# A two-layer model on one core: TensorE adds the last experts' results, tokens are mixed in the weights, and the order is written anew

## The chip, the core and the metric

The kernel runs on one core of one Trainium2 chip. A core has five engines that matter here, each with its own queue of instructions that it works off in order: TensorE (PE, matmuls and transposes), VectorE (DVE), ScalarE (ACT), GpSimd (POOL, which also issues the indirect DMAs) and SyncE (SP, which issues nearly all other DMAs). On-chip memory is SBUF, of 128 partitions; matmuls write to PSUM, of which there are eight banks of 128 x 512 float32. The metric is the time of one execution on the device in microseconds, the median of several runs.

## The reference, cut to what matters

The input x has 4 sequences of 256 tokens, each of width D = 256. Eight blocks follow one another, each adding to x what it computes from the layer-normed x. Everything is float32.

1. A "shift mix" block. With xs the sequence shifted by one token, `k = (x*tmk + xs*(1-tmk)) @ Wk.T + bk`, and in the same way v and r (r with a SiLU on the mix). A recurrence over the tokens then runs with `t = max(u+k, w)`, `e1 = exp(-w-t)`, `e2 = exp(u+k-t)`: `a = e1*a + e2*v`, `b = e1*b + e2`; its output a/b is multiplied by r and goes through Wo.
2. A mixture of 8 experts, one per token.
3. A state-space block of 8 heads.
4. The mixture of 2 again.
5. Causal attention, 16 heads in 4 groups.
6. A mixture of 32 experts, four per token: `y = (silu(x @ gate.T) * (x @ up.T)) @ down.T`, and the token's result is the sum over its four experts of weight times y.
7. Causal attention with a bias that grows with distance.
8. The mixture of 6 again.

## The kernel before, in words

The 1024 tokens form two groups of 512 (g = 0 and 1), each held in SBUF as x[g], four tiles of 128 tokens. Each block exists once per group. The blocks have letters: A shift mix, F and G the small mixture, S state space, a and b the two attentions, e and f the large mixture.

**What sets the order.** Each block is written as a set of generators ("streams"), one per kind of step, and a long string, ORDER, says which stream takes its next step: `f1d` is the `down` stream of block f, group 1, and `*3` three steps. A step is usually one instruction or a handful on one engine. As every engine is in order, the string sets the sequence on every queue, and on SP's and GpSimd's queues that of the DMAs. A second string, BANKS, says which PSUM bank each new matmul result takes. Streams are registered in `shift_mix` (L266 on), `second_ffn` (L971 on) and the main part (L1460 on).

**Normalising.** `norm_steps` (L222) runs at the head of all eight blocks for each group, so sixteen times: statistics on VectorE, a power on GpSimd (L194), then four VectorE operations (L240, one per tile: subtract the mean, multiply by the inverse deviation), eight transposes on TensorE and two copies on ScalarE.

**Shift mix.** `mix` (L288) makes three mixed inputs per group: for each of two halves of the width, ScalarE scales the shifted tokens (L294) and VectorE multiplies and adds (L296). `keys` (L302) multiplies with Wk, then two VectorE operations (L309, L312) form the two exponents, ScalarE takes the exponentials (L316, L318), and VectorE scans over the tokens (L323) and takes a reciprocal (L326). `values` (L328) scans the values (L341), and GpSimd divides (L344). `receive` (L347) multiplies by r.

**The large mixture.** `route` finds the four experts of each token and a row for each of its four copies: expert e has rows 128e to 128e+127 of a buffer in device memory. `send` (L1028) scatters the tokens' normalised rows there, sixteen indirect DMAs of 128 rows on GpSimd. The experts are worked off in sixteen pairs: `fetch` loads a pair's rows (L1060, SP), `turn` transposes them (L1069, L1073), `gate` multiplies with the gate and up weights (L199) and applies SiLU and the product (L1085, L1087), `turn_back` transposes (L1094, L1097), `down` multiplies with the down weights (L1105), copies the result to SBUF (L1109) and stores it (L1111, SP) to another buffer, `done`. When all sixteen pairs are stored, `back` (L1121) fetches for each tile of tokens the rows of its first, second, third and fourth expert, sixteen indirect DMAs per group, into six buffers that are used in turn, and `add` (L1131, VectorE) multiplies each with the token's weight and adds it to x. `leave` stores x (L1369). Buffers that not every token row reaches are filled with zeros early on (`clear`, L1399).

After the list, a check of how full the experts were chooses whether a second, general version of everything is run; with these inputs it is not.

Of the kernel before, what the change touches and what calls it, by code (L numbers as in the profile page):

```python
# [10 lines left out]
F32 = mybir.dt.float32  # L11
I32 = mybir.dt.int32
# [6 lines left out]
P = 128  # L19
D = 256  # L20
# [10 lines left out]
ROWS = E1 * CAP  # L31
NH, HP, NS = 8, 64, 64
# [7 lines left out]
x1 A0n x0 A0n x0 A0n kf*2 A1n x0*2 A0n*3 A1n x1 ls A1n A0n x1 la A0n*4 A0b A0n x1 l1 ks A0n ka  # L40
A1n*2 A0m0*2 A0n A0m1*2 ks*2 A0m0*2 ks A0m2*4 A0m1*2 la*2 A0k1 la*2 A0k1*2 A1n A0k0*3 lf*3 A1n*3
cl A1n*2 A0v0 A0k0 A0v0 cl*2 lf A0k0 A0v0*2 cl lf A0v1 A0k0*3 A1n kf*2 A1n A0m2 A1m0*2 A0k1*2 kf
lf A0v1 A1b A1n A1m0 A0v1 A1m0 A1k0 cl kf A0k1*2 A1m1*3 A0v1 A1k1 A0k1 A0v1 A1m1 lf A0r0 cl A1m2*2
A0r1 A1k1 A0v0 A0r0 A0r1 A0o*3 F0r A0o ls F0r A0o*2 F0r A0o*2 A1v0 F0r ks A1v1 F0r A1k1*3 A1k0*4
F0r*6 A1k0 A1k1 A1k0 F0r*2 A1k1 A1v0*3 A1v1 F0r*3 l1 F0r*3 A1m2*2 ls A1v1*2 k1 F0r F0s*3 A1k0 A1k1
A1m2 A1r0 F0s F0f*2 A1v0 A1r0 A1v1 A1r1*2 A1o*2 F1r A1o*4 F1r A1o*2 ls F1r*5 F0t*4 lf F0e F0f F0t
F1r*5 F0f lf F0e*3 F1r*4 F0r F1r*4 F1w F0e*2 F0t F0e F0t*2 F0e*5 ks F1s*4 F1f*2 F1t*2 F0w F0b
F1e*2 F1t F1f*2 F1e cl F0a F0b F0a S0n*2 F0b F0a F0b F1t*3 F0a F1e*2 S0n*3 F1e*4 F1t*2 F1e S0n*7
F1e k1*2 S0n S0h S0d PS S0h*2 F1e S0h*2 S0d*2 F1b F1a S1n S0d l1*2 S0h*2 S0c l1 S0h*3 S0d F1b F1a
F1b*2 F1a*2 ls S1n*4 S0g*3 S0h*3 S1n*3 S0h S0c S1n S0g*3 S0h*2 S1n S0c*2 S1n*3 S0h*2 cl S0c S0d  # L50
S0c*2 S0d F1r k1*2 S0h*4 S0c*2 S1h S0c*3 S0h*2 S0g*2 S1d*2 S0d S0u*2 S0l S1d*2 S1c l1 S0m S0u*3
S0l S0m S0l*3 S0u S0v S0m S0v S0l*3 S0v*4 S0d S0v*2 S0l S0v S1c*2 S1d*2 S0l*3 S0v S0o S0y l1 S0o
l1 S0u S0o*2 S1h S0l*2 S1h S0y*2 S0u S1d S1u S0y S0m S0l*7 S0z*3 S0l*2 S1c*2 S0z S0l S1g S1h S1g*2
S1c k1*2 S1c S1h S1c S0z*4 S1h S1c*2 S0v S0o S0z*2 S0v S1c cl*3 S1h*2 S1u cl S1h*2 S0z cl S0z*3
S1c S1h*4 S0y l1 S0y S1u S1h*2 S0z S1g S1h S0z*4 S0o S1h*4 S0y S1h S0y S0z*2 G0r*2 S0z S1h S0o S1h
S1d*2 S0o S0z S1l*2 S1m*2 S1l*6 S1m S1l S1u S1l S1v S0z S1v S0z*5 S1l*2 k1 S1u S0z*2 S1v*3 S0z*3
S1u S0z S1o S1m S0z G0r S0z*2 G0r*2 k1 S1v S1y*2 S1v G0r*3 S1v S1o*4 G0r S1l*2 S1y*2 G0r*2 S1z*2
G0r S1g S1v G0r*2 S1z*3 S1o S1z*7 G0r S1z*3 G0r*5 S1g*3 S1v S1l*2 S1z S1u S1l S1u S1l*2 S1v S1l*3
S1z*2 k1 S1z S1y*3 G0s*4 G0f S1l*2 S1y G1r G0f G0t*2 G0f S1o S1v S1o G0f S1z G0t*2 S1z G0e S1z*5
G0t*2 G0e*2 S1z*7 G0w G0e*4 G0t*2 G0e*2 S1z*3 G1r*2 G0e*2 S1z P2 G0e S1z G1r k1 G1r*3 G0b G1r*2  # L60
G0b*3 G1r G0a a0n G0a*2 a0n G1r*2 G0a a0n*2 G1r*5 a0n*5 G1r*3 G1s*4 a0n*4 a0k a0q*6 G1w a0q G1f
G0r G1r G1f a0q a0k a0p k1*2 G1t*3 G1f*2 k1 a0p*4 G1e a0p*2 G1e*2 G1t G1e a0p G1e*2 a0p*2 G1t*2
a0v*2 a0b*2 a0p*4 G1e a0w*4 a0p a0b a0w*2 a0p G1t a0w*2 a0b a0w a0c a0p*2 G1e*2 a0w*2 G1t a0f
a0p*4 G1e*3 a0f*2 a0w*3 a0c a0w*2 a0a a0w*3 a0p*2 a0f G1b a0p*4 a0f G1b a0f G1b a0w*3 a0b*2 a0w*3
G1b a0f G1a a0p a0c a0p a0b a0w*2 a0f a0w a0f a0w*3 a0c a0w G1a*2 cl a1n a0b a0w*5 a0c a0w*2 a1n
G1a a1n*3 cl a0f*3 a1n*4 a1a a1n*4 a0f a1q*3 a0f*3 a0w e0r*2 a0w*2 a1k*2 a0w*4 a1q cl lw a1q*3 a0f
lw*3 a1q a1p*5 lw*3 a0f*4 a0c a0f*3 a1b a1p a0f*4 e0r lw*4 e0r*2 a1b a1v*2 e0r*2 lw a1w*3 e0r*2
a1p*2 a1w*4 a1p*2 a1w*2 e0r*12 e0s a1p*2 e0s*4 a1c a1f*2 a1p*3 lw a1f e0s*2 a1p a1b*2 e0s a1p*2
a1w*5 a1c a1w*6 a1p*3 a1w*3 a1f*2 a1c e0s a1p*4 e0s a1f*4 e1r e0s*2 e0r e0s*3 a1p a1b*2 a1p a1w
a1f*2 a1w a1p*2 a1w a1f e0s e0f a1p e0f*2 a1w*3 a1c a1b a1w a1f a1w*7 a1c a1b a1w a1f*4 a1w*8  # L70
e0t*4 a1f*2 e0g*3 a1c e0f e0t a1f*5 e0g*2 e0t*2 a1f e0h*2 a1f e0g*3 e0h a1f e0g e1r a1f e1r*3
e0f*2 e1r*4 e0t e0g e0t*2 e0d e0f*2 e0t e0h*2 e0g*3 e0h e1r*5 e0d e1r e0d*3 e0h e0g e0h e0f e0t
e1r e0t*2 e0d*2 e0g e0h e0g e0f e1r*3 e0d*4 e0g*3 e0t*3 e0h e1r*3 e1s*6 e0h*2 e0t e0g*4 e0t*2
e0d*3 e0g*2 e0h e0g*3 e0f e0t*2 e0f*3 e0h*2 e0d*4 e0t*2 e0h e0d e1s e0h*2 e0g e1s*3 e0d e0t e0d*2
e0g e0d*2 e0g e0t e0g*2 e1s*2 e0d*2 e0h*2 e0g e0t*2 e0h*2 e0g*6 e0h e0f*2 e0d*2 e0h e0t e0g e0d
e0g e0t*3 e0d*3 e0g e0h*3 e0d*4 e0h e0d*2 e1s*4 e1f*3 e0g*2 e0h*2 e0d*3 e0g*3 e0h*2 e0d*2 e1t e0d
e1t e0d*2 e1t*2 e0d*2 e0w e0b e1g*4 e0b*2 e1h e0b e1g*2 e0b e1t*2 e1g*2 e0b e1h*3 e1f e1t e1f e1d
e1t e1g*3 e0a e1t e1d e1f*2 e1d*2 e1t e0a*2 e1t e1h e1t e1g*5 e1h*2 e1t e1h e1d e1t e1f*2 e0b
e1d*2 e1h e1d e1g e1d e0a b0n e1g*3 e1t*2 e1d e1f e0b e1h*2 e1f e1d*3 e0b*2 e1h e1d e1g e0a*4
e1g*2 e1t e1h*2 e1g e1d*2 e1t e0a e1g e0b e1d e1g*2 b0n e1t e0b e1h e1t*3 e0a e1g e0b*2 e0a*4 e1h  # L80
b0n e0b*2 e1f e1t e1f*3 e0a e1h e1g e1d*4 e1t*2 e1g e1d e0a b0n*2 e1h e1g b0n e1t e1h b0n*2 e1g*5
e1t*2 e1g b0n*2 e1f b0n e1d b0n*2 e1h b0q e1d*3 e1h*2 b0q e1h b0a b0q e1t*2 e1w e1t e1g*2 e1d*5
b0q b0k*2 e1h b0q*4 e1d e1h*2 b0p*4 e1g*3 e1d*3 e1g*2 e1d*3 e1t e1h*2 b0p*4 e1d e1g e1d*2 b0v*2
e1g*3 e1h*2 b0b*2 e1h*2 b0p e1d*7 b0w b0p*2 b0w*2 b0p*2 b0w*2 b0p*3 b0b b0p*4 b0w*4 b0b e1b e1a
b0c e1b*3 b0p*3 b0w*5 e1b b0c b0f e1a*3 b0f e1b*2 e1a e1b b0p*2 e1b*2 b0b*2 e1a b0w*3 b0f b0w
e1a*3 b0w*2 b0p*4 b0w*4 b0c e1a b0w e1b*3 b0w*5 b0f*2 e1b*2 b0f b0p b0f*4 b0b e1b b0b b0w*3 e1a
b0c b0w*2 f0r b0w*5 b0f b0c e1a*2 b0w b1n*3 b0w b0f b0w*4 e1a*3 b0f b1n*2 b0f f0r b0f*3 b1n b0c
b1n*3 b0f b1a b0f*6 b1n*3 b0f b1n b1k*2 b0f*3 f0r*2 b1q*3 f0r b1q f0r b1q*4 b1p f0r*4 b1p f0r*2
b1p*4 f0r*4 b1b*2 b1w*9 b1v f0r*3 b1p f0r*2 f0s*6 b1p*2 f0s*2 b1v b1p*2 b1c b1p f0r b1p*4 f0s
b1b*2 b1f*3 b1w*5 b1p*3 b1w*2 b1p*4 b1c f0s b1f b1w*7 f0s*2 b1p*5 f0s*2 b1c f0s b1b*2 b1f*2 f0s  # L90
f0f b1f*4 f0f b1w*9 b1c b1w*2 b1f b1w*2 b1p b1f b1p b1w b1b*2 b1w*3 f0f b1w*2 b1c b1w b1f*4 b1w*2
f0t b1f b1w b1c b1f f0w f1r*2 f0t*2 f0g f0t b1f*6 f0g*4 b1f f0h*2 f0g b1f f0t b1f f0f*2 f0t*4 b1f
f1r*3 f0h f0g*4 f0f f0d f0f*2 f1r*4 f0h*3 f0d*2 f0t f1r*3 f0d f1r*2 f0g*2 f0h f1r f0h f0d*4 f1r*3
f0g f0t*3 f1r f0d f0t*2 f0g*3 f0d*2 f0f f0g*2 f0f f0g f1r*2 f0h f0t f1s*2 f0t f0g f0h*2 f1s f0h
f0g*3 f0t*2 f0f*2 f0t*2 f1s f0d f0f f1s*4 f0d*2 f1s f0d*2 f0h f0g*4 f0f f1s*2 f1w f0g f0t*3 f0d
f0h*4 f0g*3 f0d*4 f0f f0d*2 f0t f1s f1r f0h*2 f0f f0g f0h f0t f0g*2 f0d*5 f0g*3 f0h*2 f0t*4 f0d*5
f0h f0g*2 f0t f1s*2 f0g*2 f0h f0d*2 f0g*2 f0h*4 f1s f0d f1s f1f*2 f0t f0d f0g*2 f1f f0g*2 f0d
f0h*2 f0d f0g f0d*4 f1t*2 f0h*2 f1t*2 f1g*2 f1t*2 f1g f1f*3 f0d*4 f1g*2 f0d f0b f1h f1g*2 f1h f1t
f1d f1t f1d f1t*2 f1f f1g*2 f1h f1g*4 f1h*2 f1g*2 f1d f1t*2 f1d f1t f1d f1h f1f f1h f1d f1h f0b
# [12 lines left out]
103675436254102365432651470352147634763405217364053214760765076503762145317624652436517436516742
350361501736540217653402716534071234605137201346720513764051632470562340716523471062345716324057
163240571623405763201574620153467201365247023516702357462513746251740253176253176425031425760314
# [16 lines left out]
def two_blocks(ctx: ExitStack, tc: tile.TileContext, a: dict, out: bass.AP):  # L131
# [86 lines left out]
    def chain(functions):  # L218
        for f in functions:
            yield from f()  # L220

    def norm_steps(g, name, out, dst=None):  # L222


        xg = x[g]
# [1388 lines left out]
```

## Time and profile before

| | us |
|---|---|
| median of 3 runs | 747.05 (745.83 to 756.44) |
| profiled execution, its own time | 747.44 |
| its span, first to last instruction | 745.7 |
| TensorE busy | 618.6 |
| VectorE busy | 477.7 |
| ScalarE busy | 242.4 |
| GpSimd busy | 283.4 |

The profile is of one execution. Its page gives busy times, 40 slices of the span with the busy share of each engine in tenths (9 is 90% or more) and the TensorE clock that was granted, and the costliest groups of instructions; further views give the instructions in order of time, the chain of waits that ended last, sums by window and the DMA queues. In a row such as `x8 | 65.5, 1023` the count is followed by busy microseconds and the mean nanoseconds of one. A float32 matmul appears as two instructions. L numbers are lines of the kernel before.

### The profile page before, as it was taken

To read this page: it belongs to the slowest core of one execution; us is meant where nothing else is said; L and a number is where in the kernel's file an instruction comes from. 1 tells how busy PE (TensorE), PEld (TensorE's weight loads), DVE (VectorE), ACT (ScalarE), POOL (GpSimd) and SP (SyncE) were. 2 spreads that over 40 slices of the span, in tenths; PEclk is the share of its full clock that TensorE was granted. 3 is DMA by queue.
4 is the path that set the end of the run, shared out by engine and by line. 5 is a ranking of instruction groups with operands and counts; after the bars stand their busy time and mean duration, and the time that the engine had idled before them with its cause. 6 is when DMAs were issued, how large, how long until landed. Compare 5 with 4: busy or idle time off the path is not lost. (4 is left out here: it accounts for less than half of the span.)

```text
span 745.7 us, 10482 instructions
## 1 busy us (share of the span) xinstructions
PE 618.6 (83%) x3424; PEld 430.7 (58%) x3424; DVE 477.7 (64%) x1498; ACT 242.4 (33%) x461; POOL 283.4 (38%) x333
## 2 busy tenths in 40 slices
PE   4686869998998798986899989899988889999910
PEld 1253654455666565444458978675446449989910
DVE  7898535797954567566737546458766856645642
ACT  3511214554442123521454323222432255223200
POOL 3223232342653414512730725304841660534344
PEclk9896889999999699995999999899997799999975
DMA  5842358000012123690233767322200124666643
GB/s 163 271 167 93 121 183 295 32 0 1 1 67 81 52 86 127 217 304 22 79 113 107 250 207 237 119 72 75 81 1 2 70 101 126 212 237 223 205 141 103
DMA packets 70829, 94.04 MB, mean 126 GB/s; under 512 B 6896, under 2 KB 60656, under 8 KB 70128
## 3 DMA queue, kind: packets, MB, share of 16 engines
q1 hardware_dynamic: 62944, 72.31, 30.0%
q0 software_dynamic: 7680, 20.98, 8.5%
q8 instruction: 29, 0.48, 0.3%
q14 instruction: 32, 0.26, 0.1%
q10 hardware_dynamic: 144, 0.01, 0.0%
HBM read 50.29 MB, written 42.99 MB: 125 GB/s over the span
## 5 line engine op out<-in xcount | busy, mean ns | idle before, releaser
L199 PE MATMUL pgu_f<-gu,xT_f 128*128 128x192 f32 x512 | 95.7, 333 | 1.7 <-ACT xT_f L1073 1.5
L1121 POOL DMA_INDIRECT yb_f<-done,bk_f x64 | 65.5, 1023 | 72.7 <-DVE x L1131 29.2
L1033 POOL DMA_INDIRECT sent<-xn_f,to_f x64 | 63.0, 984 | 69.0 <-DVE to_f L1021 33.5
L199 PEld LDWEIGHTS pgu_f<-gu,xT_f 128*128 128x128 f32 x512 | 85.0, 194 | 4.6 <-ACT xT_f L1073 3.4
L1105 PE MATMUL py_f<-dw,hT_f 96*128 96x256 f32 x256 | 65.9, 386 | 3.4 <-DVE hT_f L1097 3.4
L1109 DVE COPY ye_f<-py_f 128x512 f32<-128x512 f32 x64 | 43.6, 687 | 28.7 <-PE py_f L1105 18.1
L853 DVE CUSTOM_DVE_ANT_0 junk_a<-pS_a,tri 128x128 f32<-128x128 f32 (+1 forms) x128 | 45.7, 357 | 22.6 <-PE pS_a L843 16.6
L1073 ACT COPY xT_f<-px_f 128x512 f32<-128x512 f32 x64 | 36.8, 587 | 53.3 <-PE px_f L1069 41.8
L853 DVE CUSTOM_DVE_ANT_0 junk_b<-pS_b,tri 128x128 f32<-128x128 f32 (+1 forms) x128 | 45.7, 357 | 12.8 <-PE pS_b L843 6.1
L1105 PEld LDWEIGHTS py_f<-dw,hT_f 96*128 96x128 f32 x256 | 45.4, 192 | 9.3 <-DVE hT_f L1097 4.6
L1085 ACT ACTIVATE he_f<-pgu_f 128x192 f32<-128x192 f32 x64 | 21.2, 332 | 83.9 <-PE pgu_f L199 70.0
L1131 DVE SCALAR_TENSOR_TENSOR x<-yb_f,wt_f,x 128x256 f32<-128x256 f32 x64 | 31.8, 503 | 23.5 <-DMA yb_f<-done,bk_f 22.9
L1087 DVE TENSOR_TENSOR he_f<-he_f,pgu_f 128x192 f32<-128x192 f32 x64 | 22.3, 348 | 28.6 <-ACT he_f L1085 28.5
L891 POOL TENSOR_SCALAR_AFFINE_SELECT pT_b<-pT_b 128x512 f32<-128x512 f32 x32 | 20.6, 672 | 49.5 <-ACT pT_b L888 49.4
L888 ACT ACTIVATE pT_a<-pST_a 128x512 f32<-128x512 f32 x48 | 25.6, 605 | 42.4 <-PE pST_a L880 41.0
L1069 PE MATMUL px_f<-ident,xe_f 128*128 128x128 f32 x256 | 36.9, 273 | 1.6 <-DMA xe_f<-sent 1.6
L1097 DVE COPY hT_f<-ph_f 96x256 f32<-96x256 f32 x64 | 26.1, 415 | 17.5 <-PE ph_f L1094 15.8
L199 PE MATMUL py_f<-W,xT_f 128*128 128x256 f32 x128 | 34.6, 421 | 3.1 <-ACT xT_f L489 3.1
L888 ACT ACTIVATE pT_b<-pST_b 128x512 f32<-128x512 f32 x48 | 25.4, 604 | 30.8 <-PE pST_b L880 25.2
L891 POOL TENSOR_SCALAR_AFFINE_SELECT pT_a<-pT_a 128x512 f32<-128x512 f32 x32 | 19.6, 644 | 37.9 <-ACT pT_a L888 37.9
L1069 PEld LDWEIGHTS px_f<-ident,xe_f 128*128 128x128 f32 x256 | 30.6, 141 | 5.6 <-issue 2.9
L194 POOL TENSOR_TENSOR rstd_f<-var_f,neghalf 128x4 f32<-128x4 f32 x8 | 8.2, 1024 | 66.4 <-DVE var_f L233 66.3
(294 smaller groups left out, 1297.1 us busy)
## 6 DMA issues: line engine op xcount, KB each, us to landing
xe_f<-sent SPq DMA_DIRECT2D x64, 256.0 KB, 3.2
done<-ye_f SPq DMA_DIRECT2D x64, 256.0 KB, 2.5
sent<-nil SPq DMA_DIRECT2D x16, 512.0 KB, 7.8
xe_f<-fsent SPq DMA_DIRECT2D x16, 256.0 KB, 2.9
fdone<-ye_f SPq DMA_DIRECT2D x16, 256.0 KB, 2.1
gu<-in_L1f_gate SPq DMA_DIRECT2D x4, 768.0 KB, 12.8
gu<-in_L1f_up SPq DMA_DIRECT2D x4, 768.0 KB, 17.9
dw<-in_L1f_down SPq DMA_DIRECT2D x4, 768.0 KB, 17.4
```

Of the source, the lines that this page charges most:

```text
L199: nc.tensor.matmul(dst, w(c), rhs(c), start=(c == 0), stop=(c == n - 1))
L853: nc.vector.tensor_tensor_reduce(out=junk[:, :w], in0=four[s][:, at:at + w], in1=tri[:, S - w:], scale=1.0, scalar=NEG, op0=ALU.add, op1=A ...
L888: nc.scalar.activation(pT.rearrange("p c q -> p (c q)"), pS, AF.Exp)
L891: nc.gpsimd.affine_select(pT, pT, pattern=[[0, AG], [1, P]], compare_op=ALU.is_ge, fill=zero, base=0, channel_multiplier=-1)
L1033: nc.gpsimd.indirect_dma_start(out=sent_to[g][t * TOPK + j], out_offset=bass.IndirectOffsetOnAxis(ap=to[:, t, j:j + 1], axis=0), in_=xn[:, ...
L1069: nc.tensor.transpose(px[:, j * P:(j + 1) * P], xe[q][:, k, c * P:(c + 1) * P], ident)
L1073: nc.scalar.copy(xT[q].rearrange("p k c t -> p (k c t)"), px)
L1097: nc.vector.tensor_copy(hT[q].rearrange("p k t -> p (k t)"), ph[:, :2 * P])
L1105: nc.tensor.matmul(py[:, k * D:(k + 1) * D], hT[q][:, k, :], dw[:, 2 * q + k, :], start=True, stop=True)
L1109: nc.vector.tensor_copy(ye.rearrange("p k d -> p (k d)"), py)
L1121: nc.gpsimd.indirect_dma_start(out=yb, out_offset=None, in_=done[g], in_offset=bass.IndirectOffsetOnAxis(ap=kept_["back"][:, t, j:j + 1], ...
L1131: nc.vector.scalar_tensor_tensor(x[g][:, t, :], due[t, j], kept_["wt"][:, t, j:j + 1], x[g][:, t, :], ALU.mult, ALU.add)
```

## The change

It has four parts.

1. **Last group's last eight experts.** `second_ffn` gets an argument `end`; for block f, group 1 it is 8. There, tokens are sent with nine more numbers in their row: the token's number, its four experts and their four weights (buffer `end_sent`, 265 wide). `fetch` also loads those numbers for the rows of experts 24 to 31. `claim` makes from them, for each of the eight experts, a matrix of 128 rows by 512 tokens that holds the weight where the row belongs to the token. The results of pairs 12 to 15 are not stored; `collect` multiplies these matrices with them on TensorE, summed over the eight experts in two PSUM banks, and two VectorE operations add the sums to x. `back` and `add` stay; a copy that went to experts 24 to 31 fetches a row of zeros behind the others (`end_done`).
2. **First block.** The mixing of k and v is moved into the weights: `share` makes tmk*Wk and (1-tmk)*Wk (the same for v) once, on ScalarE, and `mixed` multiplies the tokens with the first and the shifted tokens with the second, four matmuls in place of two. `mix` remains for r. The two exponents are formed by ScalarE as Relu, with changed constants, in place of VectorE.
3. **Normalising.** The four VectorE operations become four of ScalarE with scale and bias; a small VectorE operation makes the bias.
4. **The list.** ORDER and BANKS are new throughout, and the new buffers are zeroed by a new stream, `ce`.

```diff
 def norm_steps(g, name, out, dst=None, xn=None):
+        shift = small.tile([P, NT], F32, tag="shift", name=f"shift_{name}")
+        nc.vector.scalar_tensor_tensor(shift, mv[:, :, 0], -1.0, rstd, ALU.mult, ALU.mult)
...
-            nc.vector.tensor_scalar(
-                xn[:, t, :], xg[:, t, :], mv[:, t, 0:1], rstd[:, t:t + 1],
-                ALU.subtract, ALU.mult)
+            nc.scalar.activation(xn[:, t, :], xg[:, t, :], AF.Identity,
+                                 bias=shift[:, t:t + 1], scale=rstd[:, t:t + 1])
...
+        def mixed(dst, w2, es):
+            xp = kept_["xp"]
+            dst = dst.rearrange("p (b s) -> p b s", b=2)
+            for i, t in enumerate(w2):
+                for c in range(NC):
+                    nc.tensor.matmul(dst, t[:, c, es], xp[:, c, :, 1 - i:S + 1 - i],
+                                     start=(i + c == 0), stop=(i + c == NC))
...
-            nc.vector.tensor_scalar(
-                flat(low), pk, bkuw[:, e:e + 1], 0.0, ALU.add, ALU.min)
-            nc.vector.tensor_scalar(
-                flat(top), pk, bku[:, e:e + 1], w[:, e:e + 1], ALU.add, ALU.max)
+            nc.scalar.activation(flat(low), pk, AF.Relu, bias=minus[:, e:e + 1], scale=-1.0)
+            nc.scalar.activation(flat(top), pk, AF.Relu, bias=bkuw[:, e:e + 1])
...
+                if end and q == 2:
+                    nc.sync.dma_start(
+                        info, sent_[through * 2 * CAP:, D:].rearrange("(k p) d -> p k d", k=end))
...
-                nc.sync.dma_start(rows(done[g], q), ye)
+                if q < through:
+                    nc.sync.dma_start(rows(done_, q), ye)
...
+        def claim():
+            nc.vector.tensor_tensor(
+                mine, info[:, :, 1:1 + TOPK],
+                iota[:, E1 - end:].unsqueeze(2).to_broadcast([P, end, TOPK]), ALU.is_equal)
+            nc.vector.tensor_tensor(mine, mine, info[:, :, 1 + TOPK:], ALU.mult)
+            nc.vector.tensor_reduce(sw, mine, AX.X, ALU.add)
+            for i in range(end):
+                nc.vector.tensor_scalar(
+                    to, numbers, info[:, i, 0:1], sw[:, i, :], ALU.is_equal, ALU.mult)
...
+        def collect():
+            two = [bank(k, f"pend_{name}_{k}") for k in ("acc", "st")]
+            for i in range(end):
+                q, k = through + i // 2, i % 2
+                for t in range(NT):
+                    nc.tensor.matmul(
+                        two[t // 2][:, t % 2 * D:(t % 2 + 1) * D],
+                        due["to", i][:, t * P:(t + 1) * P], due["ye", q][:, k, :],
+                        start=(i == 0 and t % 2 == 0), stop=(i == end - 1 and t % 2 == 1))
+            for t in range(0, NT, 2):
+                xt = x[g][:, t:t + 2, :]
+                nc.vector.tensor_tensor(
+                    xt, two[t // 2].rearrange("p (k d) -> p k d", k=2), xt, ALU.add)
...
+        def share(i, whole, part):
+            for t, by in ((part, tm), (whole, omt)):
+                for c in range(NC):
+                    nc.scalar.activation(t[:, c, :], whole[:, c, :], AF.Copy, scale=by[:, c, i:i + 1])
```

The end of the old list, from the last steps of group 1's products on, and of the new one:

```diff
-... f1h*2 f0b f1d*5 f0a*5 f0b f0a f0b f0a f0b
-f0a f1b*2 z0 f1a*2 f1b f1a f1b*3 f1a*2 z0*3 f1b*2 f1a*3 z1*2 f1b f1a f1b*4 f1a*3 z1 f1a f1b*3
-f1a*3 z1
+... f1d f1g*3 f1h*2 f1t
+f1g*3 f1h*2 f1d*4 f1c*2 f1d f1c f1g*2 f1h f1c f1m*3 f1h*2 f0a f1d*2 f1h f1m f1c f0a f1c f1b*2 f1d
+f1m*2 f1d f1m*3 f1b f1a*3 f1b f1a f1m f1b f1a f1b f1a f1b*5 z1 f1b f1r f1a*6 f1b f1a f1b f1a f1b
+f1a f1b z1*2 z0*2 f1a z1
```

`f1m` is `collect` (eight steps of four matmuls, then the two additions), `f1c` is `claim`, `f1b` a fetch of `back`, `f1a` an addition of `add`.

## The prediction

> **What bounds the kernel now.** First the busy shares in 40 slices of 18.6 us:
>
> ```profile
> PE   4686869998998798986899989899988889999910
> DVE  7898535797954567566737546458766856645642
> PEclk9896889999999699995999999899997799999975
> ```
>
> Three regions: a first block (slices 1 to 6) in which TensorE is half idle and VectorE is the busiest engine; a long middle in which TensorE is at 8 or 9 tenths; and a tail of almost two slices without any matmul. The tail is read from the timeline (start, length, engine, line, operation):
>
> ```profile
> 696.81 1.89 PE L1105 MATMUL py_f<-dw,hT_f 96*128 96x256 f32 x8
> ...
> 711.53 1.13 PE L1105 MATMUL py_f<-dw,hT_f 96*128 96x256 f32 x4 [0.51 <-DVE hT_f L1097]
> 712.70 0.69 DVE L1109 COPY ye_f<-py_f 128x512 f32<-128x512 f32 x1 [0.63 <-PE py_f L1105]
> ...
> 718.21 1.00 POOL L1121 DMA_INDIRECT yb_f<-done,bk_f  x1 [1.59 <-DMA out<-x]
> 719.52 1.00 POOL L1121 DMA_INDIRECT yb_f<-done,bk_f  x1 [0.30 <-issue]
> ...
> 738.08 1.01 POOL L1121 DMA_INDIRECT yb_f<-done,bk_f  x1 [0.30 <-issue]
> ...
> 740.93 0.48 DVE L1131 SCALAR_TENSOR_TENSOR x<-yb_f,wt_f,x 128x256 f32<-128x256 f32 x1 [0.61 <-DMA yb_f<-done,bk_f]
> ```
>
> The last matmul ends at 712.66; then the last results are stored, and sixteen gathers follow at one per 1.31 us. The chain of waits closes it:
>
> ```profile
> 738.08 2.76 DMA yb_f<-done,bk_f
> ...
> 740.93 0.48 DVE x L1131
> ```
>
> A gather takes 2.76 us to land, its addition 0.48, and from 741.41 the output store and the close take 4.3 us to 745.7. Tail: 745.7 - 712.66 = 33.0 us. For the first block I read the sums by window (engines in the order PE, PEld, DVE, ACT, POOL; then clock, DMA share, GB/s) and its timeline:
>
> ```profile
> 25.00:50.00 25.00, 18.07 (x45) 8.64 (x43) 23.26 (x35) 7.64 (x12) 4.43 (x4) 0.86 0.82 275
> 50.00:75.00 25.00, 17.00 (x54) 10.94 (x53) 21.27 (x43) 5.75 (x9) 6.64 (x6) 0.73 0.21 72
> ```
>
> ```profile
> 20.15 1.37 DVE L240 TENSOR_SCALAR xn_a<-x,mv_a,rstd_a 128x256 f32<-128x256 f32 x4
> 21.74 3.60 PE L199 MATMUL pv<-mix,wv 128*128 128x512 f32 x8
> 31.15 6.95 PE L199 MATMUL pk<-mix,wk 128*128 128x512 f32 x8 [5.37 <-DVE mix L296]
> 61.92 6.56 DVE L326 RECIPROCAL sb<-sb 128x512 f32<-128x512 f32 x2
> ```
>
> VectorE has 23 and 21 of 25 us; matmuls wait for its mix.
>
> **Tail, removed and added.** Removed: the stores and fetches of the last four pairs, not the sixteen gathers. All sixteen stay; rows of experts 24 to 31 are merely replaced by one zero row. But they may start when pair 11 is stored. Added on TensorE: 8 experts x 4 tiles x 2 instructions (an f32 matmul shows as two) = 64 of 256 columns. The row at 696.81 gives 1.89/8 = 0.236 us each in a stream: 15.1 us. From below it cannot be less while TensorE is full (25.0 of 25 us busy from 675 to 700); from above each could cost its mean latency, 0.386 us by the group's row: 24.7. I take 0.236, since the rows in question also load a new weight per matmul. Two idle gaps before the last matmuls (0.76 and 0.51 us) get filled. The last matmul, E, moves to 712.66 + 15.1 - 1.3 = 726.5.
>
> What comes after E is decided by order. In the changed program VectorE has: last result copied, first addition of the TensorE sums (waits for the last matmuls), then the sixteen additions of fetched rows. VectorE is in order, and there are six fetch buffers. Six gathers can go early: pair 11's product ends about 25 us before E (three gate groups 4.4, four products 4.1, small transposes, 15.1 of sums), its store lands some 3.5 us on, so they are all done before E. The seventh needs the buffer of the first, whose addition is queued behind the TensorE sums. So the added wait, on VectorE, holds ten gathers on GpSimd. After E: the addition (0.69, begun 0.5 before E, when its bank is complete), 0.48 for the first fetched row: E + 0.7; the tenth gather issued 9 x 1.31 later, E + 12.5; landing 2.76, add 0.48, close 4.3: E + 20.1 = 746.6, against 745.7. **Tail: +0.9 us.** TensorE's 15.1 eats what leaves the tail. Bounds: 0 to +10.5.
>
> **First block.** Off VectorE: 8 mixes x 0.74 = 5.9, 8 key operations of 0.75 and 0.80 = 6.2, four norms x 1.38 = 5.5: 17.6 us. Onto ScalarE: 8 Relu of about 0.72 (the row of mixtmp, L294) for 8 mixtmp taken off; 8 weight scalings and the norms at 0.38 to 0.48 each (ScalarE's 128x256 rows, L933 and L749). ScalarE has 6 to 11 of 25 us there. Onto TensorE: 16 more products of two instructions. By the row at 21.74 an instruction is 3.60/8 = 0.45 us: 14.4; by the row at 31.15, 0.87: 27.8. [...] I take 0.45 to 0.6: 14 to 19 us in a stretch where TensorE has 7 to 8 us idle per 25.
>
> On the chain, mixtmp 0.72 and mix 0.74 go and twice the product (1.8) comes: nothing. What can gain is only VectorE's queue. I followed it through the new order: group 0 leaves attention some 2.5 us sooner, but the second reciprocal of group 1 now stands behind group 0's routing, as the pair at 61.92 did, so group 1 gains 2; and before the state space starts, two expert products stand between its two sets of transposes. Between 0 and -10; I take **-2**, nearest to that walk.
>
> **Norms.** All sixteen: four VectorE operations (1.38) become a small one (0.17) and four of ScalarE (1.5 to 1.9), with one more handoff (about 0.2): +0.5 to +0.95 until the transposes, and behind an exponential (0.605, L888) up to +1.55. In the trace TensorE waited before transposes at 7 of 17 places; elsewhere other work hides it. 7 x 0.75 = 5, less what the freed VectorE returns: **+2** (from -5 to +10). ScalarE also gets four more table loads in the new order (26 for 22), most of them in the state-space stage, 1.28 each in the trace; 5.1 on an engine about half busy there: **+1** (0 to 5).
>
> **A new wait: the token numbers.** The load of 1024 pieces of 36 bytes stands on SP's queue behind the first three fetches of the last group. VectorE's claim waits for it, and behind the claim stand that group's first gate products, for which TensorE's transposes wait. The queue's line
>
> ```profile
> q1 hardware_dynamic: 62944, 72.31, 30.0%
> ```
>
> gives 0.30 x 16 x 745.7 / 62944 = 57 ns of one engine per packet, so 1024/16 x 57 = 3.6 us. [...] Bounds 0 and 5; I take the row's price and **+1**.
>
> **Covered edits.** Clearing the wider send buffer (4.3 MB, nine DMAs) stands on SP's queue before the expert weights. At the best slice's 304 GB/s that is 14 us more. The weights were issued from 304 us on, 9.4 MB or some 31 us, and first used at 382.4: about 47 us of cover; without it, 14. Claims: 8 x about 0.6 on VectorE, which has 9 us free of 25 there; at worst 6. Sends with rows of 1060 bytes instead of 1024, two iotas and casts: nothing. The result: +0.9 - 2 + 2 + 1 + 1 = +2.9 on the profiled 747.44, whose span is 745.7 (the median of three runs, 747.05, is next to it): **750**. The new list rearranges everything else. Between 125 and 700 us TensorE's idle time sums to 56 us; a fair list could win or lose some 8 of it, and I put the mean at nothing.
>
> **Rivals.**
> - *VectorE set the pace.* If the first block passes on 12 of its 17.6, and twelve later norms a third of their 1.2 each (5): 747.4 + 0.9 - 17 = 731. For it: 23.3 of 25 us busy at 25 to 50, 23.4 at 150 to 175. Against: the order of reciprocals, and TensorE's own 14 to 19 there.
> - *Slower: norms wait in ScalarE's queue.* Place: the head of every stage. Price: 1.55 each with an exponential in front. It passes 2% from ten exposed norms on (15.5); with twelve, 18.6: 747.4 + 0.9 - 2 + 1 + 1 + 18.6 = 767. Against: only 7 places waited.
> - *Gathers hidden after all.* If fetched rows were added before the TensorE sums, only the two additions of the sums and the close would follow E, some 5.2 us: 731.7, and with the other +2 and the 1.7 us that lie outside the span 735. The order on VectorE speaks against it; it lies within 2% anyway.
>
> **Numbers.** Forecast, little change, 0.65 (738 to 762); hidden gathers 0.05; VectorE's pace 0.12; ScalarE's queue 0.18. So faster than 2% 0.12, within 0.70, slower 0.18; 2% is about what a measurement of this kernel can tell from no change. Range 735 to 763: it reaches into both outer cases, with the list's 8 and the bounds of norms and first block.
>
> **What would show it.** Last matmul about 14 us later than 712.66; 64 new matmul rows 0.236 us apart; exactly six gathers of the last group before E, ten after it 1.31 apart; end about 20 us after E; VectorE's windows at 25 to 75 down by some 10 us while the first state-space transposes still come near 111. Wrong if the early stages end over 10 us sooner, if TensorE waits before most transposes, or if the gathers run on past E without a pause.

## The result, and the profile after

The changed kernel takes 773.83 us (median of 4 runs, 771.93 to 778.76), the kernel before 750.5 (4 runs, 745.83 to 756.44). The ratio is 1.0345, with a 95% interval of 1.0293 to 1.0396: slower by some 25 us, where 750 was forecast. The profiled execution took 771.93 us, its span is 770.2, 24.5 more than before.

The busy tenths of the changed kernel's page, in slices of 19.3 us, first:

```profile
PE   5968679899998699695989989899997999989990
DVE  3786336487564456647635755658948645645753
PEclk9989789699999699997899999998997599989995
```

VectorE is indeed less busy in the first slices (3 7 8 6 for 7 8 9 8), and the tail without matmuls is now one slice instead of two. Both things happened that the change does on purpose, and still the end is later. The windows view, cut at the same events in both kernels (the last product of the first small mixture; the first transpose of the last group's experts; the last matmul), shows where. The columns are the time on PE, PEld, DVE, ACT and POOL with instruction counts, then granted clock, share of DMA, GB/s. Before:

```profile
0.00:113.40 113.40, 76.29 (x254) 48.69 (x255) 80.34 (x187) 31.15 (x46) 32.31 (x46) 0.85 0.50 166
113.40:611.50 498.10, 443.08 (x2542) 291.07 (x2541) 326.09 (x1127) 177.45 (x342) 200.80 (x237) 0.93 0.32 104
611.50:712.70 101.20, 99.23 (x632) 90.98 (x630) 59.23 (x161) 33.76 (x73) 31.68 (x32) 1.00 0.60 193
```

After:

```profile
0.00:114.50 114.50, 85.04 (x290) 53.09 (x291) 62.60 (x155) 44.24 (x75) 31.84 (x45) 0.90 0.39 136
114.50:630.00 515.50, 455.48 (x2539) 295.23 (x2538) 317.39 (x1102) 203.11 (x385) 202.67 (x241) 0.91 0.36 115
630.00:749.40 119.40, 115.96 (x696) 105.32 (x694) 66.60 (x180) 35.13 (x77) 39.94 (x40) 0.97 0.55 171
```

| stretch | before | after | change | forecast |
|---|---|---|---|---|
| to the last product of the first small mixture | 113.4 | 114.5 | +1.1 | -2 |
| from there to the last group's experts of block f | 498.1 | 515.5 | +17.4 | +3 (norms 2, table loads 1) |
| those experts and the TensorE sums | 101.2 | 119.4 | +18.2 | +14.8 |
| tail behind the last matmul | 33.0 | 20.8 | -12.2 | -12.9 |
| span | 745.7 | 770.2 | +24.5 | +2.9 |

So the forecast missed by 21.6 us, and 14.4 of them are in the middle, a stretch in which the change touches the norms and the list and, beside them, only the clears and the wider rows that are sent. TensorE has nearly the same instructions there (2542 and 2539) but is busy 12.4 us longer at a lower clock (0.91 for 0.93), and idle 5.0 us longer (55.0, now 60.0).

The tail, in the changed kernel's timeline (start, length, engine, line, operation, idle before and its releaser):

```profile
733.83 1.28 POOL L1198 DMA_INDIRECT yb_f<-end_done,bk_f  x1 [6.22 <-DVE ye_f L1148]
...
742.12 1.07 POOL L1198 DMA_INDIRECT yb_f<-end_done,bk_f  x1 [1.75 <-DVE x L1208]
...
748.42 1.03 PE L1181 MATMUL pend_f_st<-ye_f,cw_f 128*128 128x256 f32 x4
748.62 0.69 DVE L1188 TENSOR_TENSOR x<-pend_f_acc,x 128x512 f32<-128x512 f32 x1 [5.35 <-PE pend_f_acc L1181]
749.35 2.05 DVE L1208 SCALAR_TENSOR_TENSOR x<-yb_f,wt_f,x 128x256 f32<-128x256 f32 x4
750.11 1.13 POOL L1198 DMA_INDIRECT yb_f<-end_done,bk_f  x1 [6.92 <-DVE x L1208]
...
762.04 1.17 POOL L1198 DMA_INDIRECT yb_f<-end_done,bk_f  x1 [0.30 <-issue]
```

Six gathers go between 733.83 and 742.12, GpSimd then stands 6.92 us, and ten follow from 750.11, 1.3 apart. VectorE stands 5.35 us before the first addition of the sums with those fetched rows ready behind it. Three rows of the chain of waits:

```profile
119.48 8.66 DMA yb_f<-fdone,bk_f
...
310.77 6.36 DMA yb_f<-fdone,bk_f
...
762.04 3.30 DMA yb_f<-end_done,bk_f
```

It closes as it did before. Its first two rows are gathers of the second group in the first and in the second small mixture; before, the four in each place took 5.7 to 6.6 and 2.8 to 3.8 us to land. The chain of the kernel before leads back only to 734.87, so whether gathers lay on it earlier can't be read.

### The profile page after: what moved, and what is told of

It is laid out like the page before. It is cut to its first block, busy times and chain, and to the rows that moved or that the text cites. A ratio compares the mean times of both kernels' runs of the same rounds, so it can differ in the third digit from the quotient of the medians.

```text
span 770.2 us, 10750 instructions
## 1 busy us (share of the span) xinstructions
PE 656.5 (85%) x3520; PEld 453.6 (59%) x3520; DVE 455.1 (59%) x1455; ACT 282.5 (37%) x537; POOL 284.8 (37%) x335
## 3 DMA queue, kind: packets, MB, share of 16 engines
q1 hardware_dynamic: 67634, 75.65, 30.2%
## 4 chain that ended last, share of the span: by engine, by line
PE 50%; DVE 18%; issue 10%; DMA 9%; ACT 8%; POOL 4%; POOLq 0%; SPq 0%; DVEq 0%; ACTq 0%
PE pgu_f L204 8%; PE py_f L1144 6%; DMA yb_f<-fdone,bk_f 3%; PE px_f L1108 3%; PE pST_b L894 2%; DVE junk_a L867 2%; PE py_f L204 2%; PE pST_a L894 2%; PE pq_a L204 2%; PE pS_b L857 2%; DVE junk_b L867 2%; PE pctx_b L916 2%; PE pctx_a L916 2%; PE po_a L204 2%; PE pob L204 1%
## 5 line engine op out<-in xcount | busy, mean ns | idle before, releaser
L204 PE MATMUL pgu_f<-gu,xT_f 128*128 128x192 f32 x512 | 93.9, 330 | 0.3 <-ACT pT_a L902 0.3
L1198 POOL DMA_INDIRECT yb_f<-done,bk_f x48 | 49.6, 1034 | 58.2 <-DVE x L1208 20.3
L1068 POOL DMA_INDIRECT sent<-xn_f,to_f x48 | 47.3, 985 | 49.2 <-issue 27.9
L1148 DVE COPY ye_f<-py_f 128x512 f32<-128x512 f32 x64 | 43.7, 686 | 29.2 <-PE py_f L1144 16.8
L1208 DVE SCALAR_TENSOR_TENSOR x<-yb_f,wt_f,x 128x256 f32<-128x256 f32 x64 | 31.5, 499 | 13.8 <-DMA yb_f<-end_done,bk_f 7.6
L1136 DVE COPY hT_f<-ph_f 96x256 f32<-96x256 f32 x64 | 26.2, 415 | 21.3 <-PE ph_f L1133 19.4
L905 POOL TENSOR_SCALAR_AFFINE_SELECT pT_a<-pT_a 128x512 f32<-128x512 f32 x32 | 19.7, 638 | 44.9 <-ACT pT_a L902 44.9
## 6 DMA issues: line engine op xcount, KB each, us to landing
gu<-in_L1f_gate SPq DMA_DIRECT2D x4, 768.0 KB, 13.5
```

The costliest lines, as they stand in the source:

```text
L204: nc.tensor.matmul(dst, w(c), rhs(c), start=(c == 0), stop=(c == n - 1))
L905: nc.gpsimd.affine_select(pT, pT, pattern=[[0, AG], [1, P]], compare_op=ALU.is_ge, fill=zero, base=0, channel_multiplier=-1)
L1068: nc.gpsimd.indirect_dma_start(out=sent_to_[t * TOPK + j], out_offset=bass.IndirectOffsetOnAxis(ap=to[:, t, j:j + 1], axis=0), in_=xn[:, t ...
L1148: nc.vector.tensor_copy(ye.rearrange("p k d -> p (k d)"), py)
L1198: nc.gpsimd.indirect_dma_start(out=yb, out_offset=None, in_=done_, in_offset=bass.IndirectOffsetOnAxis(ap=kept_["back"][:, t, j:j + 1], ax ...
L1208: nc.vector.scalar_tensor_tensor(x[g][:, t, :], due[t, j], kept_["wt"][:, t, j:j + 1], x[g][:, t, :], ALU.mult, ALU.add)
```

## The experiments

All were timed beside the kernel before on the same chip, and a ratio is to that kernel. Two of the chips used took 802 and 803 us for the kernel before, not 750, so their ratios are compared only with each other. Where a part is put into the old list, its new steps stand where the new list or the data allow, and the PSUM banks are those of the old list.

### One part at a time in the old list

Norms on ScalarE, with everything else as before:

```diff
-            nc.vector.tensor_scalar(xn[:, t, :], xg[:, t, :], mv[:, t, 0:1], rstd[:, t:t + 1], ALU.subtract, ALU.mult)
+            nc.scalar.activation(xn[:, t, :], xg[:, t, :], AF.Identity, bias=shift[:, t:t + 1], scale=rstd[:, t:t + 1])
```

> The kernel before with one thing done: norms on ScalarE, the small operation put into the old list just ahead of them; old first block, old tail. Theory N: 757 to 767 us. Theory L: 745 to 752. My recorded sum had +2 for it, 749.

Measured: 778.48 us, ratio 1.0394 (1.0267 to 1.0521), above theory N's 757 to 767 too. This one edit alone costs as much as the whole change. As the list is the same, each matmul can be set against its twin, and one jump of the lag is 6.0 us at a single place. Before, around the norms of block e, group 1:

```profile
390.90 0.58 ACT L1073 COPY xT_f<-px_f 128x512 f32<-128x512 f32 x1
...
391.56 1.54 PE L199 MATMUL pgu_f<-gu,xT_f 128*128 128x192 f32 x8
```

and with the norms on ScalarE:

```profile
415.09 1.04 POOL L197 TENSOR_TENSOR rstd_f<-var_f,neghalf 128x4 f32<-128x4 f32 x1 [10.86 <-DVE var_f L236]
416.16 0.16 DVE L241 SCALAR_TENSOR_TENSOR shift_f<-mv_f,rstd_f 128x4 f32<-128x4 f32 x1 [1.15 <-POOL rstd_f L197]
...
416.36 2.07 ACT L247 ACTIVATE xn_f<-x,shift_f,rstd_f 128x256 f32<-128x256 f32 x4 [4.01 <-DVE shift_f L241]
418.34 0.56 ACT L1104 COPY xT_f<-px_f 128x512 f32<-128x512 f32 x1
...
418.95 2.93 PE L202 MATMUL pgu_f<-gu,xT_f 128*128 128x192 f32 x8 [5.88 <-ACT xT_f L1104]
```

The copy needed nothing from the norm: its transposed tokens had lain ready since 410. It stood behind the norm in ScalarE's queue while ScalarE waited 4.01 us for VectorE and GpSimd, and TensorE stood 5.88 us; the matmuls behind ran at half pace (2.93 for 1.54). Before, the first operation behind this norm on VectorE was a copy (L1097), and TensorE did not wait for it.

The same edit, but with each norm's four operations as late in ScalarE's queue as they can stand (in the second group of both attentions they so come behind the addition of the block's bias to x and normalise another x, so that the result is another one; the instructions are as many as before):

```diff
-e1r*4 e0t e0g e0t*2 e0d e0f*2 e0t e0h*2 e0g*3 e0h e1r
+e0t e0g e0t*2 e0d e0f*2 e0t e0h*2 e0g*3 e0h e1r*5
```

> The kernel before with the norms on ScalarE, as in the earlier run, but the four operations of each norm as late in ScalarE's queue as they can stand, directly before the norm's transposes, so that copies which TensorE waits for go first. Theory Q (waiting work behind the norms): the two places that gave 4.1 and 6.0 us of the 31 vanish, ratio to the kernel before 1.022 to 1.030 instead of 1.039. Theory D (only the norm's own length counts): 1.035 to 1.045.

Measured: 764.08 us, ratio 1.0198 (1.0123 to 1.0272), on theory Q's side and a little below its band. Half of the price went away with the place in the queue, more than the two places named. Lag of the last transpose of some norms behind the kernel before, in us (third row: the doubled norm of the next section):

| time before | 52.9 | 134.2 | 254.3 | 336.3 | 397.2 | 481.0 | 565.0 | 625.5 |
|---|---|---|---|---|---|---|---|---|
| norms on ScalarE | 7.8 | 13.0 | 13.5 | 21.3 | 29.9 | 27.0 | 32.7 | 31.6 |
| the same, late | 4.3 | 6.7 | 7.2 | 15.8 | 16.8 | 16.0 | 19.7 | 18.2 |
| VectorE's norms twice | 9.8 | 12.4 | 17.6 | 24.4 | 26.7 | 25.4 | 30.2 | 31.6 |

The lag grows in steps spread over the program, and little of it is won back. These are profiled executions; that of the late placement (766.56 us) was the longest of its four, and by the medians it loses 14 us, not 18.

The first block alone (the scalings in the places of the mixes of k and v, their weights loaded sooner):

```diff
-A1n*2 A0m0*2 A0n A0m1*2 ks*2 A0m0*2 ks A0m2*4 A0m1*2 la*2
+A1n*2 kk*2 A0n kv*2 ks*2 kk*2 ks A0m*4 kv*2
```

> The kernel before with only the new first block (mixing in the weights, Relu on ScalarE), put into the old list: the weight scalings stand where the mixes of k and v stood. Theory F (the first block's doubled products move later stages back by more than VectorE gains): 752 to 758 us. My recorded sum: -2, so 745; the recorded bound of a gain is 737. Theory L: between 740 and 748.

Measured: 751.56 us, ratio 1.0046 (1.0014 to 1.0078): +3.4 us, neither a gain nor the loss of theory F.

The new end alone:

```diff
+    if end and q == 2: nc.sync.dma_start(info, ...)
-    nc.sync.dma_start(rows(done[g], q), ye)
+    if q < through: nc.sync.dma_start(rows(done_, q), ye)
+streams[n + "c"] = claim(); streams[n + "m"] = collect()
```

> The kernel before with only the new end of the last group (rows with token numbers, claim, collect, sixteen gathers of which experts 24 to 31 fetch a zero row), put into the old list near the same steps as in the new one. Recorded sum: +0.9 for the tail and +1 for the token numbers, so 749; last matmul near 727, end 20 us after it. If instead the last experts' stretch lengthens by 18 us as it did in the changed kernel (119.4 for 101.2), 753.

Measured: 767.32 us, ratio 1.02 (1.0081 to 1.032), worse than the sum. Its wide clears ran at 295 to 310 us, and there the gathers of the second small mixture took 5.9 to 7.7 us (before: 2.8 to 3.8). With the clears early, and the last gathers and their additions laid among the last products:

```diff
-cl ce*9
+ce*9 G0f
...
-f1d f1m f1c*2 f1d f1m*2 f1d f0a*5 f0b f0a f0b f0a f0b f0a f1b*2 f1m*3 f1b f1a*3 f1b
+f1a f1b f1a f1b f1d f1m f1c*2 f1a f1b f1d f1m*2 f1a f1b f1d f1m*2 f1a f1b
```

> The kernel before with the new end of the last group in its old list, the gathers interleaved with the last products as above, and the wide buffer cleared early, near 120 us, instead of at 295. From 747: TensorE's added 15.9 and some 2 of drift, less the tail that shrinks from 33 to about 12: 742 to 748. If the clears at 295 to 315 us were not what delayed that kernel's middle (its lag grew from 2.8 to 9.8 us there): 748 to 756.

> The kernel before with the new end of the last group alone, gathers interleaved, early clears. On the slow chip it reached the third block's norms at the time of the kernel before (330.7 for 331.8 us). Theory: the tail alone, placed so, is worth a little: 740 to 747, up to 1% below the kernel before. If TensorE's 16 us eat it all: 747 to 752.

Measured on the slow chips: ratios 0.9965 (0.9919 to 1.0011) and 0.9982 (0.993 to 1.0034). Placed well, the new end costs nothing and brings nothing that can be told from no change. It is the best version found, and it does not beat the kernel before. Early clears and interleaved gathers were not tried apart.

All three parts in the old list, clears early:

> All three parts of the change in the old list (norms on ScalarE, new first block, new end as in the changed kernel, clears early). If the parts add up (3.9% for the norms, 0.5% for the first block, 0 to 2% for the end): ratio 1.045 to 1.065, and the new list of the changed kernel (1.0345, and 1.019 on the slow chip) has won back 1 to 4% of it. If instead the new list is what costs: ratio 1.00 to 1.03.

Measured: 791.08 us, ratio 1.0548 (1.0463 to 1.0632). The parts add up (3.9 + 0.5 + 0 to 2), and the new list with the same parts is at 1.0345. So for these parts the new list is not the cause of the loss: it wins two points back. With norms on VectorE it does not win, as shown below.

### How open a norm's time is

The norm's four operations twice, with the same result:

```diff
+            nc.scalar.activation(xn[:, t, :], xg[:, t, :], AF.Identity, bias=shift[:, t:t + 1], scale=rstd[:, t:t + 1])
             yield
```

> The changed kernel with each normalising operation of ScalarE issued twice (same result): 64 more of 0.55 to 0.59 us, 2.3 us per norm, 37 in all. Theory N (the norm's time on ScalarE lies open at most of the sixteen places): 25 to 40 us slower, 799 to 813. If it is covered at most places, as my recorded sum had it (7 of 16): 10 to 17 us, 784 to 791. Theory L, norms next to nothing: under 8, below 781.

> The kernel before with each normalising operation of VectorE issued twice: 64 more of 0.345 us at full pace, 1.4 us per norm, 22 in all. If a norm's time is as open before as after the change: 15 to 24 us slower, 763 to 772. With 7 of 16 open: 10, 757.

Measured: the changed kernel goes to 829.27 us (ratio 1.1088, 1.0907 to 1.1269), 55 more; the kernel before goes to 779.1 (1.0412, 1.0288 to 1.0536), 29 to 31 more. Both are above what was expected of fully open norms (799 to 813 and 763 to 772). How much longer one norm became has to be read from its rows. VectorE, before and doubled (first and last of eight rows):

```profile
7.57 1.38 DVE L240 TENSOR_SCALAR xn_a<-x,mv_a,rstd_a 128x256 f32<-128x256 f32 x4 [0.17 <-POOL rstd_a L194]
...
7.43 0.41 DVE L240 TENSOR_SCALAR xn_a<-x,mv_a,rstd_a 128x256 f32<-128x256 f32 x1 [0.17 <-POOL rstd_a L194]
...
10.20 0.41 DVE L243 TENSOR_SCALAR xn_a<-x,mv_a,rstd_a 128x256 f32<-128x256 f32 x1
```

ScalarE, changed and changed with doubled norms:

```profile
76.82 2.08 ACT L249 ACTIVATE xn_f<-x,shift_f,rstd_f 128x256 f32<-128x256 f32 x4 [2.39 <-DVE shift_f L243]
...
85.99 0.60 ACT L249 ACTIVATE xn_f<-x,shift_f,rstd_f 128x256 f32<-128x256 f32 x1 [2.39 <-DVE shift_f L243]
...
90.00 0.60 ACT L251 ACTIVATE xn_f<-x,shift_f,rstd_f 128x256 f32<-128x256 f32 x1
```

On VectorE the four operations went from 1.38 us to 3.18: 1.80 more, not the 1.38 that was expected: the eight operations start 0.40 us apart on the mean (10.20 - 7.43 over seven), not 0.345. Sixteen times that is 28.8 us, and the kernel takes 29 to 31 longer, so on the whole a lengthening is paid once, in full. On ScalarE they went from 2.08 to 4.61, sixteen times 40.5, and the time grew by 55, 1.4 us for each. So the norms as a whole are covered in neither kernel; that not a single one is covered isn't shown. What the changed kernel pays on top goes with a lower clock: over the stretch to the last matmul it is granted 0.92 and with doubled norms 0.88, and TensorE's busy time goes from 656.5 to 681.6 us for the same instructions.

### Norms back on VectorE in the new list

> The changed kernel with one thing undone: the four normalising operations of each norm are VectorE's again (the step of the small operation is empty); new list, new first block, new tail. Theory N (the norms on ScalarE cost the 18 us that the body lost): 756 to 762 us, and the first matmuls of the last experts near 615 instead of 630. Theory L (the new list costs them, the norms next to nothing): 768 to 776, the last experts' first matmuls at 626 or later.

Measured: 781.7 us, ratio 1.0401 (1.0289 to 1.0513), slower than theory N and L alike expected. The list had put the norm's steps where ScalarE was free, and on VectorE other work came between them: one norm ended 13.5 us after GpSimd began its power and another 8.3, where the kernel before has 2.5 at most places. So the steps were moved together (theory N below still takes 1.4 us of time for each us of a norm; the rows above give about 1.0 for VectorE's):

```diff
-S1n S0h*2 S1n*2 k1*2 S1n*2 S0c*3 ls S0g
+S1n*5 S0h*2 k1*2 S0c*3 ls S0g
```

> The changed kernel with the norms back on VectorE as in the run before, and besides the four operations of each norm directly behind one another at the place of the small operation (in the earlier run they stood where the list had put them for ScalarE, and VectorE's own work came in between). Theory N (a norm's length lies open at every place, at 1.4 us of total time per us): norms shorter by 1.0 to 1.5 us at sixteen places, 752 to 762 us. Theory L (the new list is slow by itself): 768 to 782.

> Norms on VectorE and close together, in the new list. On the slow chip it brought the last matmul 5.5 us forward against the kernel with norms on ScalarE there. Theory N in full (all of the body's 18 us are the norms'): 752 to 758. Norms a third of it and the new list the rest, as the slow chip's trace has it: 764 to 770.

> The changed kernel itself, as the measure for the three runs beside it on this chip: on the chip of the last four runs the kernel before took 803 us, and the changed kernel had not been run there. 770 to 775 where the kernel before takes 745 to 755.

Measured on the slow chips: 1.0114 (1.003 to 1.0198) and 1.0091 (1.0046 to 1.0137); the changed kernel itself on the second of them 812.18 us, 1.019 (1.0097 to 1.0283). Undoing the norms so takes back half of the loss there, but the intervals overlap, and on the other slow chip, in the next section, it takes nothing back.

### Gathers, clears, clock

The last group's additions laid among the last products of the changed kernel, all else the same, and both edits together:

```diff
-f0a f1d*2 f1h f1m f1c f0a f1c f1b*2 f1d f1m*2 f1d f1m*3 f1b f1a*3 f1b
+f1d f1a f1b f1a f1b f1d f1h f1m f1c*2 f1a f1b f1a f1b f1d f1m*2 f1d f1m*2 f1a f1b
```

> The changed kernel with only its last steps in another order: the additions of the last group's fetched rows stand among the last products instead of behind the first addition of the TensorE sums, so that the gathers run on from 734 us without a pause; 16 at 1.31, 2.8 to land, addition and close: end of the span at 761. Theory H (the order on VectorE held ten gathers): 9 us faster, 761 to 766. If the gathers are held by something else: 771 to 775.

> Gathers interleaved with the last products, all else as changed. On the slow chip the end came 14.9 us after the last matmul instead of 20.8. Theory H: 6 to 9 us below the changed kernel, 763 to 767. Else the same as it.

> Both changes of the two runs before together. Theories N and H: 742 to 752. L and H: 759 to 772. N without H: 752 to 762.

Measured: 1.0034 (0.9986 to 1.0081), 1.0138 (1.0049 to 1.0228) and 1.0114 (1.0036 to 1.0191), in this order; the first and third on one slow chip, the second on the other, where the changed kernel had 1.019. The first and third differ in the norms alone. With norms on VectorE the sixteen stretches from the start of GpSimd's power to the last normalised tile sum to 54.0 us in the timeline, with norms on ScalarE to 69.7; yet the shorter norms gained nothing (1.0114 against 1.0034), which is outside what theories N and H together allow. On the same chip the old list with norms on VectorE, the old first block and the same end was at 0.9965. So with norms on VectorE the new list, with its late clears and the new first block (0.5% alone), costs 1.5 points.

Theory H's mechanism is plain in the timeline of the second:

```profile
793.74 1.01 POOL L1197 DMA_INDIRECT yb_f<-end_done,bk_f  x1 [0.30 <-DVE x L1207]
...
795.82 0.68 DVE L1187 TENSOR_TENSOR x<-pend_f_acc,x 128x512 f32<-128x512 f32 x1
...
800.28 1.01 POOL L1197 DMA_INDIRECT yb_f<-end_done,bk_f  x1 [0.30 <-DVE count L1600]
```

GpSimd no longer stands at the last matmul (795.6); four more gathers follow and the span ends at 810.4, 14.8 us after it instead of 20.9 in the changed kernel beside it. The total can't show these 6 us well: the last matmul itself came at 795.6 here and at 785.7 there.

The last three clears of the wide buffer moved to about 131 us:

> The changed kernel with the last three zeroing DMAs of the wide send buffer (they ran at 249.8, 300.2 and 304.8 us) moved to right behind the others, near 131 us. Theory Z (they delay the second small mixture's last gathers, which took 5.4 to 6.6 us at 308 to 312 where before they took 2.8 to 3.8, and the attention behind them): gathers back to 2.8 to 3.8 us and 3 to 5 us faster, 768 to 771. Theory L (the list sets the time, other work takes the wait's place): 773, within 2.

Measured: 773.34 us, ratio 1.0358 (1.0191 to 1.0526), no gain, and two of the late gathers still took 4.7 and 5.9 us. They were not the only writers: in the new list twelve clears of 512 KB of the other buffers are issued between 291 and 311 us, where the kernel before issues three. Theory Z may have named the wrong clears; moving the twelve was not tried.

Six transposes of the identity ahead of each norm's transposes, so that TensorE doesn't stand still:

```diff
             pt = mm_tile(f"pt_{name}_{c}")
+            for _ in range(6 if c == 0 else 0):
+                nc.tensor.transpose(pt[:, :P], ident, ident)
```

> The changed kernel with six TensorE transposes of the identity put ahead of each norm's transposes (overwritten by them), so that TensorE is not idle while it waits for the norm; about 1.5 us of work per norm, 24 in all at full clock if none of it fell into idle time. Theory C (idle before the norms' transposes drops the granted clock, and the half-clock stretches, 123 us against 106 before, make the body slow): half-clock time back to about 106 us or less and no slower than 773, 765 to 773. If the clock does not hang on these gaps: 778 to 795.

Measured: 770.84 us, ratio 1.0287 (1.0142 to 1.0432). Ninety-six more instructions cost no time that can be measured, and the clock over the whole run was granted at 0.916 where the changed kernel's was 0.909. That is inside what theory C expected; a gain isn't shown. What the clock does behind one norm is seen in windows of 8 us over the second set of state-space norms, with the row of the transposes or of sixteen products below them. Before:

```profile
132.00:140.00 8.00, 8.00 (x19) 3.48 (x20) 6.98 (x21) 5.04 (x10) 1.15 (x2) 0.79 0.03 9
140.00:148.00 8.00, 8.00 (x36) 4.43 (x34) 4.45 (x8) 4.34 (x8) 3.96 (x4) 1.00 0.00 0
148.00:156.00 8.00, 6.84 (x38) 4.69 (x37) 7.04 (x11) 4.84 (x8) 4.66 (x4) 1.00 0.00 0
...
131.99 2.19 PE L249 MATMUL pt_b<-ident,xn_b 128*128 128x128 f32 x8 [3.10 <-DVE xn_b L240]
...
142.30 1.85 PE L199 MATMUL pd<-win,xnT_b 128*128 128x8 f32 x16
```

After:

```profile
132.00:140.00 8.00, 4.27 (x14) 1.70 (x12) 5.90 (x18) 6.43 (x13) 5.86 (x8) 0.95 0.69 222
140.00:148.00 8.00, 7.89 (x21) 4.66 (x22) 3.03 (x9) 1.17 (x3) 0.00 (x0) 0.50 0.00 0
148.00:156.00 8.00, 8.00 (x27) 5.96 (x26) 4.35 (x8) 3.57 (x7) 2.05 (x2) 0.50 0.00 0
...
143.72 3.58 PE L204 MATMUL pd<-win,xnT_b 128*128 128x8 f32 x16
```

After the change TensorE is idle 3.7 of the first 8 us, while the norm and then the copy of its transposes are on ScalarE, and for the next 16 it works almost without a gap at half the clock: the same sixteen products take 3.58 us there, 1.85 before. But before, TensorE had stood 3.10 us for this norm too, just ahead of the windows, and the half clock behind that lasted only some 3.4 us (0.79 over the first window; in narrower ones 0.95 from 132 to 133 us, 0.50 from 133 to 136 and 0.92 from 136 to 138). So the idle time alone doesn't say how long the half clock lasts, and what does stays open.

## Why the prediction was wrong

**Tail: right.** Six early gathers, ten behind the last matmul at 1.31, end 20.8 us after it (forecast 20.1), held by VectorE's order; new_hidden_2 took the order away, and GpSimd's pause with it.

**Last experts: mechanism right, 3.4 us short.** The sums ran from 733.5 to 749.4, but among other work: their rows of four stand 0.86 us apart, 13.8 in all, less than the 15.1 worked out. In the whole stretch TensorE is busy 16.7 us longer and idle 1.5 longer. The 4.4 us beside the sums aren't isolated. The trace shows one wait of 2.6 us for a fetch of the wide rows (3.6 us from issue to landing on the page, against 3.0 for the narrow ones) and a clock of 0.97 where it had been 1.00. The +1 us put down for the token numbers no run shows: their load is issued at 685.04, the first operation on them (691.14) follows at once on a copy at 690.53 before which VectorE had stood 6.27 us, by the profile for the store of a result, and no wait for the numbers is among TensorE's longest.

**First block: no gain came.** -2 was forecast, within 0 to -10; it was +1.1 in the trace (with four of the norms in it) and +3.4 alone in the old list. TensorE was busier there (85.0 us for 76.3) and the clock rose from 0.85 to 0.90; whether the one brought the other no run shows. The 36 added instructions lengthened TensorE's busy time by 8.7 us, less than the 14 of the sum (other stages' edges move across the cut too). The 0.6 us that the prediction allowed for one of them was the author's estimate, which no run shows: the 64 instructions of k and v are busy for 31.3 us in the changed kernel, 0.49 each, and the 32 before for 19.6. VectorE lost 18.0 - 9.3 = 8.7 us in the first window and only 4.3 in the two for which 10 were named.

**Norms: the step that failed.** It was put at +2; alone in the old list it cost 3.9%, some 29 us, and 14 when placed late. The price of one was right: where nothing else interferes, as at the first attention's first norm (with norms on ScalarE in the old list transposed 4.7 us after GpSimd's power began, before 3.9), it is +0.9, within the 0.5 to 0.95 given. Two other things were not. First, "in the trace TensorE waited before transposes at 7 of 17 places; elsewhere other work hides it": a missing wait before the transposes was read as cover. (There are sixteen norms, and by the timeline TensorE stood more than 0.2 us before or between the transposes of eight; the 7 seem to leave out the 3.10 us before a state-space norm's transposes, shown above.) The doubled norms show no cover on the whole: 29 to 31 us more for 28.8 added. Routing, gating and projections follow the norm in a chain; that TensorE runs out of other work there instead of before the transposes is the likely reason, not traced place by place. Without cover the forecast's own price makes 16 x 0.9 = 14 us, the size that the late placement measured. The agreement is one of size: there several norms also stood behind other work on ScalarE. Second, the new wait was not followed to the queue behind it. The prediction asked what the norm waits for on ScalarE (an exponential, up to 1.55); the runs show what waits behind the norm while ScalarE waits for VectorE and GpSimd: in the old list that doubled the price, from 1.98% to 3.94%.

**Rivals.** "Slower: norms wait in ScalarE's queue" (767, chance 0.18) named the edit that costs most in the old list and nearly the right time, by a queue seen from one end: there other work waits behind the norms. "VectorE set the pace" falls, since VectorE is freed by 22.6 us in all (477.7 to 455.1) and the middle gets longer.

**Clears: cover misjudged, worth little alone.** The cost was put at nothing because weights would arrive in time. The gathers that ran beside clears took longer (8.66 and 6.36 us on the chain), but moving some of the clears gave nothing.

**The new list.** Put at nothing with 8 us to either side. Against the same parts in the old list it is worth about 1.0548 - 1.0345, two points or 15 us. By these two ratios the parts cost more than the middle's 17.4 us, and the list pays some back. How the 17.4 split between norms and the rest within the new list stays open: lengthened norms cost it dearly, but norms put back on VectorE gave 1.009 for 1.019 on one slow chip and 1.0114 for 1.0034 on the other. So the norms are shown as the cause in the old list; in the changed kernel they are not. The four added table loads (26 for 22 in the trace, 1.28 us each) were not tried alone.

## What to carry to other kernels

Before moving an operation to an idle engine, list what stands behind it in that engine's queue: if its inputs come late, everything ready behind it waits with it, and this cost as much here as the slower operation (3.94% in all, 1.98% with the norms late in the queue). That the matmul engine shows no wait at a step does not mean that the step is covered: double it, read from the rows how much longer it became (here 1.80 us, not 1.38), and see what the total does. That a longer step costs time does not mean that a shorter one gives it back. An order fitted to one placement can be a bad one for another, so a part is judged best in both lists.

## What the runs showed of the hardware

- TensorE stayed at half clock for 16 us while the profile shows it busy almost without a gap (7.89 and 8.00 of 8 us, clock 0.50 in both windows). Before the change the half clock behind the same norm lasted some 3.4 us (0.50 from 133 to 136 us, 1.00 again from 138 to 140). What sets the length no run shows.
- A row of four normalising operations took 2.07 us on ScalarE and 1.38 on VectorE (0.52 and 0.345 each), more than the 0.38 to 0.48 taken from ScalarE's copies of the same size.
- Chips differ: two took 802 and 803 us for the kernel before. In the changed kernel on one of them VectorE stands in places for several us with no engine of the core named:

```profile
377.79 0.42 DVE L867 CUSTOM_DVE_ANT_0 junk_a<-pS_a,tri 128x256 f32<-128x256 f32 x1 [4.30 <-remote]
...
450.92 0.42 DVE L1136 COPY hT_f<-ph_f 96x256 f32<-96x256 f32 x1 [6.82 <-remote]
```

What it waits for there the trace doesn't say. The profiles of the kernel before and after on the first chip have no such wait, so the ratios of the slow chips may hold a share of it.
